# Moving one projection of an attention layer forward in a hand-ordered program, and two products of a hidden layer ahead of their two Relus

## The chip, the core and the metric

The kernel runs on one core of one Trainium2 chip. The metric is the device time of one execution in microseconds; lower is better. TensorE (PE in the profile) multiplies matrices into PSUM, VectorE (DVE) and ScalarE (ACT) read PSUM and work on SBUF, GpSimd (POOL) works on SBUF and issues some transfers, SyncE (SP) issues the other ones. Each engine runs its instructions in the order in which the program was written for it.

## What is computed

Eight sequences of 512 rows and 256 features go through two blocks. The first is a state-space layer: a projection to 512 channels, a short convolution, a recurrence over time with 16 states per channel, a gate and a projection back. The second is an attention layer of 16 heads whose values and outputs pass through 8 experts, of which the gates let 2 through, followed by a layer of 1024 hidden units (called the net below). In the reference, cut to what the change touches:

```python
q = _rope(einsum('bsd,hdp->bhsp', x, Wq))      # 16 heads of 64
k = _rope(einsum('bsd,hdp->bhsp', x, Wk))
v = einsum('bsd,bhse,hedp->bhsp', x, _gate(x, Wsel_v), Wv)
att = softmax(einsum('bhsp,bhtp->bhst', q, k) / sqrt(64))
o = einsum('bhst,bhtp->bhsp', att, v)
src2 = einsum('bhsp,bhse,hepd->bsd', o, _gate(x, Wsel_o), Wo)
...
src2 = relu(src @ W1 + b1) @ W2 + b2           # the net
```

`_rope` turns 32 of a head's 64 features by an angle that depends on the row: each feature is multiplied by a cosine, and a partner feature, multiplied by a sine, is added.

## The kernel before

**Work units.** Heads are taken in pairs, 8 pairs for each of the 8 sequences, 64 in all; pair 3.6 below is pair 6 of sequence 3. A pair consists of these parts, in the kernel's own numbering:

- the projection of q and k (`project`, L631): 8 matmul records on PE (L638). Then `turned` (L645) makes two products of its result on DVE, one with the sines (tile `sin`) and one with the cosines (tile `qk`), and `rotate` (L656) issues four transfers from POOL (L660) that add the rows of `sin` onto their partner rows of `qk`.
- v0 to v3 (`values`, L724): 8 matmul records each (L735). DVE multiplies the result by the gates into a tile `ve`, and POOL adds the eight experts up in three instructions (L750 to L752).
- s0 to s3 (`scores`, L667): 4 matmul records each (L676), which need the finished `qk`. DVE takes the row maximum (`low`), ACT the two exponentials (L691), DVE the reciprocal of the sum, ACT the scaling (L700).
- t0 to t3 (`turn_over`, L705): 8 transposes each (L711), copied out by ACT (L717).
- o (`attend`, L757): 16 matmul records (L764), which need all t and all v of the pair. ACT copies the result, and DVE multiplies it by the output gates in four steps (tile `og`, L785).
- a0 to a7 (`add_output`, L787): 4 matmul records each (L803), the output projection of the pair before. a0 and a1 need the first `og`, a2 and a3 the second, and so on.

**Order.** PE, DVE, ACT and POOL run exactly in the order in which the Python program emits their instructions. The attention parts are emitted in the list of `ahead` (L905); `following` in that list calls `follow` (L897), which emits the projection of q and k for the next pair. At the last pair of a sequence, `follow` first runs the planner until the next sequence is in `state` (L901): this is set (L599) when the last DVE instruction of `best(0)`, which makes the value gates `gv`, has been emitted.

After each part `order_of.run()` (class `_Order`) emits what has come due. Parts of the state-space layer, of the gates and of the net are generators that yield a waiting time; the planner counts PE time as the parts state it (`pe(3.42)`) and DVE time by the number of columns, and lets such a part go ahead while DVE is planned to be free at least 0.5 us before the next due step. ACT and POOL are not counted. The planner knows nothing of waits for buffers.

**Buffers.** All PE results except the output projection go into three PSUM buffers of `[128, 2, 512]` that are handed out in turn (`banks`, L274): a part may start to write when the reader of the third part before it is done. In SBUF there are two buffers in turn for each tag of the pool `work`. The four probability tiles `p` of a pair and `sin` share the tag "p"; the four `ve` tiles have the tag "ve". `qk` and `v` have one buffer.

**The net.** `feed_forward` (L812) takes the sequence before while the attention of the next one runs. Its hidden layer has 4 tiles of two products each per sequence (L853). Each product is followed by its Relu on ACT (L858), which writes half of tile `h`, and the part then yields 6.0. Two tiles are followed by the product with W2 (L868).

Of the kernel before, what the change touches and what calls it, by code (L numbers as in the profile page):

```python
# [25 lines left out]
F32 = mybir.dt.float32  # L26
# [5 lines left out]
P = 128  # L32
B, S, D = 8, 512, 256
# [6 lines left out]
NF = F // P  # L40
# [49 lines left out]
class _Order:  # L90
# [10 lines left out]
    def pe(self, us):  # L101
        self.now += us
        self.here = self.now
# [9 lines left out]
    def then(self, us, do):  # L113

        heapq.heappush(self.queue, (max(self.here, self.vec) + us, self.n, do))
        self.n += 1
# [84 lines left out]
def _layers(  # L201
# [4 lines left out]
    with ExitStack() as ctx:  # L206
# [6 lines left out]
        work = pool("work", 2)  # L213
# [60 lines left out]
        def banks(name):  # L274
            return psum.tile([P, 2, S], F32, tag="mm", name=name)

        def to_features(to, frm, name):

            ps = banks(f"ps_tr_{name}")
            for c in range(ND):  # L280
                for t in range(NT):
                    nc.tensor.transpose(ps[:, c, bass.ts(t, P)], frm[:, t, bass.ts(c, P)], ident)
            nc.scalar.copy(to, ps)
# [8 lines left out]
        pe, after, then = order_of.pe, order_of.after, order_of.then  # L292
# [324 lines left out]
        class Pair:  # L617
# [25 lines left out]
                after(0.05, lambda: self.turned(ps))  # L643

            def turned(self, ps):  # L645
                self.sin = work.tile([P, 2, S], F32, tag="p", name=f"sin_{self.id}")
                vector.tensor_tensor(
                    self.sin, ps, angle[:, 1].to_broadcast([P, 2, S]), ALU.mult
                )
                self.qk = one.tile([P, 2, S], F32, tag="qk", name=f"qk_{self.id}")  # L650
                vector.tensor_tensor(
                    self.qk, ps, angle[:, 0].to_broadcast([P, 2, S]), ALU.mult
                )
                then(0.0, self.rotate)
# [157 lines left out]
        def feed_forward(b, pa):  # L812

            xt, _ = state.pop(b)
            acc = big.tile([P, ND, S], F32, tag="big", name=f"acc_{b}")
            vector.tensor_tensor(acc, xt, pa, ALU.add)
            summed.add(b)
            yield 0.1
            while b + 1 < B and not (b + 1 in gated and (b + 2 == B or b + 2 in scanning)):
                yield 1.0  # L820
            ps = banks(f"ps_acc_{b}")
            ps = ps.rearrange("p a (t d) -> p (a t) d", d=D)
            for t in range(NT):
                for c in range(ND):
                    nc.tensor.transpose(ps[:, t, bass.ts(c, P)], acc[:, c, bass.ts(t, P)], ident)
            pe(1.05)
            y = big.tile([P, NT, D], F32, tag="big", name=f"y_{b}")
            nc.scalar.copy(y, ps)
            yield 1.2
            yield from norm(y, [y[:, t, :] for t in range(NT)])  # L830
            vector.tensor_tensor(y, y, g1, ALU.mult)
            yield 0.0
            vector.tensor_tensor(y, y, o1, ALU.add)
            yield 0.1
            yt = big.tile([P, ND, S], F32, tag="big", name=f"yt_{b}")
            to_features(yt, y, f"f_{b}")
            pe(1.05)
            yield 1.2
            b2 = half.tile([P, 1, D], F32, tag="half", name=f"b2_{b}")
            nc.sync.dma_start(out=b2[:, 0, :], in_=rows[:, 4 * D :].to_broadcast([P, D]))  # L840
            vector.tensor_tensor(y, y, b2.to_broadcast([P, NT, D]), ALU.add)

            for k in range(2):
                w = big.tile([P, ND, F // 2], F32, tag="big", name=f"w1_{b}_{k}")
                nc.sync.dma_start(out=w, in_=w1[:, :, k * F // 2 : (k + 1) * F // 2])
                hid = []
                for f in range(0, NF // 2, 2):
                    ps = banks(f"ps_f1_{b}_{k}_{f}")
                    h = big.tile([P, 2, S], F32, tag="big", name=f"hid_{b}_{k}_{f}")
                    for i in range(2):  # L850
                        at = k * NF // 2 + f + i
                        for c in range(ND):
                            nc.tensor.matmul(  # L853
                                ps[:, i, :], lhsT=w[:, c, bass.ts(f + i, P)], rhs=yt[:, c, :],
                                start=(c == 0), stop=(c == ND - 1),
                            )
                        pe(1.71)
                        nc.scalar.activation(  # L858
                            h[:, i, :], ps[:, i, :], AF.Relu, bias=b1_t[:, at : at + 1]
                        )  # L860
                    hid.append(h)
                    yield 6.0
                w = big.tile([P, NF // 2, D], F32, tag="big", name=f"w2_{b}_{k}")
                nc.sync.dma_start(out=w, in_=w2[:, k * NF // 2 : (k + 1) * NF // 2, :])
                ps = banks(f"ps_f2_{b}_{k}").rearrange("p a (t d) -> p (a t) d", d=D)
                for t in range(NT):
                    for f in range(NF // 2):
                        nc.tensor.matmul(  # L868
                            ps[:, t, :], lhsT=hid[f // 2][:, f % 2, bass.ts(t, P)], rhs=w[:, f, :],
                            start=(f == 0), stop=(f == NF // 2 - 1),  # L870
                        )
                    pe(1.71)
                    if t == 1:
                        yield 0.0
                yield 0.1
                vector.tensor_tensor(y, y, ps, ALU.add)
                yield 4.0
            z = big.tile([P, NT, D], F32, tag="big", name=f"z_{b}")
            x1 = big.tile([P, NT, D], F32, tag="big", name=f"x1_f_{b}")
            nc.sync.dma_start(out=x1, in_=x1_d[b])  # L880
            yield from norm(z, [y[:, t, :] for t in range(NT)])
            vector.tensor_tensor(z, z, g2, ALU.mult)
            yield 0.0
            vector.tensor_tensor(z, z, o2, ALU.add)
            yield 0.0
            yield from norm(z, [z[:, t, :] for t in range(NT)])
            vector.tensor_tensor(z, z, x1, ALU.add)
            nc.sync.dma_start(out=out[b].rearrange("(t p) d -> p t d", p=P), in_=z)
            finished.add(b)
# [15 lines left out]
        def ahead(n, following):  # L905


            for part in (
                "v0", "s0", 0, 1, "v1", "s1", 2, 3, "t0", "s2", "v2", "t1", "s3", 4, 5, "v3", "t2",
                following, 6, "t3", 7,  # L910
            ):
                if isinstance(part, int):
                    if last:
                        last.add_output(part)
                elif isinstance(part, str):
                    {"v": n.values, "s": n.scores, "t": n.turn_over}[part[0]](int(part[1]))
                else:
                    part()
                order_of.run()

        last = None
        with tc.manual_schedule(engines=MANUAL):
            first = front(0)
            order_of.start(first, 0, next(first))
            order_of.start(mamba(0), 0)
            first_constants()
            order_of.run(lambda: 0 in scanning)
            order_of.start(later_constants(), NET)
            order_of.run(lambda: 0 in state)
            pairs = {}  # L930
            follow(-1, H // 2 - 1)
            for b in range(B):
                for pair in range(H // 2):
                    now = pairs.pop((b, pair))
                    ahead(now, lambda: follow(b, pair))
                    if pair == 0 and b:
                        order_of.start(feed_forward(b - 1, sums[b - 1]), NET)
                    order_of.run(lambda: b in gated)
                    now.attend()
                    order_of.run()  # L940
                    last = now
            for k in range(E):
                last.add_output(k)
                order_of.run()
            order_of.start(feed_forward(B - 1, sums[B - 1]), NET)
            order_of.run(lambda: not (order_of.queue or order_of.rest))
# [83 lines left out]
```

## Time and profile before

| | us |
|---|---|
| runs shown: median (lowest to highest) | 3807.0 (3799.87 to 3809.49) |
| the profiled execution's own time | 3804.05 |
| its span, first to last instruction | 3802.3 |
| PE busy in the span | 3362.9 |
| DVE busy | 3049.0 |
| ACT busy | 1657.2 |
| POOL busy | 1656.8 |

The mean granted TensorE clock is 0.942 of full speed. A row of the groups names the line, the engine, the operation, what it writes and reads and how often it ran, then the busy time with the mean duration of one in ns, and then how long the engine had been idle just before these instructions and what ended that. In the view of waits a row is one kind of wait: who waited for whom, the sum, how often, and the longest. In a timeline, a row is a run of like instructions: start, length, engine, line, operation, and in brackets the idle time before it. All DVE instructions have the line of the helper that counts them (L160), so on DVE one goes by tile names.

The steps of an undisturbed pair, as the timeline shows them with PE at full clock: 3.4 us for a v part or the projection of q and k, 1.06 for an s part, 0.87 for a t part, 1.72 for an a part, 3.58 for o.

### The profile page before, as it was taken

The numbers are of one execution on the slowest core, as the hardware profiler recorded it, in microseconds if no ns is written. First come the engines' busy times: TensorE is split into PE (matmuls) and PEld (weight loads), VectorE is DVE, ScalarE is ACT, GpSimd is POOL, SyncE is SP. The second block draws the span as 40 slices with busy tenths as digits, with TensorE's granted clock in tenths as the row PEclk, the third lists the DMA queues.
The fourth block names the chain that finished last, engine by engine and source line by source line (L and its number), as shares of the span: only waits on it lengthen the run. The fifth ranks groups of instructions, "written<-read, shape, count | busy, mean of one in ns | idle before, by whom it ended". The sixth has DMA issues, their size and how long they took to land.

```text
span 3802.3 us, 33611 instructions
## 1 busy us (share of the span) xinstructions
PE 3362.9 (88%) x10464; PEld 1560.0 (41%) x10464; DVE 3049.0 (80%) x3218; ACT 1657.2 (44%) x2761; POOL 1656.8 (44%) x1601
## 2 busy tenths in 40 slices
PE   2039999399989999999999999999999999999996
PEld 0023444244444444444444444444444444444443
DVE  6976899799879888799878988799888989664432
ACT  4216654144544446444563446334463435332331
POOL 1323466255534545345443554445453557332220
PEclk6569999699999999999999999999999999999998
DMA  5934778368755867468674877557683777443431
GB/s 164 202 63 128 176 188 194 84 168 192 179 146 139 189 168 192 119 160 195 160 187 106 195 173 190 141 145 187 162 208 91 182 193 180 116 111 101 120 94 56
DMA packets 287760, 584.19 MB, mean 154 GB/s; under 512 B 37848, under 2 KB 125144, under 8 KB 287584
## 3 DMA queue, kind: packets, MB, share of 16 engines
q1 hardware_dynamic: 205664, 431.00, 38.3%
q0 software_dynamic: 81920, 151.04, 24.5%
q8 instruction: 85, 1.39, 0.1%
q14 instruction: 91, 0.75, 0.1%
HBM read 409.39 MB, written 21.51 MB: 113 GB/s over the span
## 4 chain that ended last, share of the span: by engine, by line
PE 57%; DVE 21%; DMA 7%; ACT 6%; issue 6%; POOL 3%; SPq 0%; DVEq 0%; POOLq 0%; ACTq 0%
PE ps_a L803 16%; PE ps_v L735 14%; DVE h L160 8%; PE ps_s L676 5%; PE ps_o L764 3%; PE ps_pt L711 3%; PE ps_f L853 3%; DMA xc<-h 3%; PE ps_qk L638 3%; PE ps_f L868 3%; DVE og L160 2%; DMA qk<-sin 2%; DVE ve L160 2%; PE ps_out L511 2%; DVE low L160 1%
## 5 line engine op out<-in xcount | busy, mean ns | idle before, releaser
L750 POOL TENSOR_TENSOR ve<-ve 128x512 f32<-128x512 f32 x256 | 420.2, 1641 | 1348.6 <-DVE ve L160 1248.0
L803 PE MATMUL ps_a<-og,wo 128*128 128x512 f32 x2048 | 978.5, 617 | 11.6 <-DVE og L160 11.2
L735 PE MATMUL ps_v<-wv,xt 128*128 128x512 f32 x2048 | 935.2, 599 | 3.8 <-ACT p L691 3.8
L160 DVE TENSOR_TENSOR_SCAN h<-da,h 128x1024 f32<-128x1024 f32 x256 | 609.7, 2382 | 87.1 <-ACT da L440 74.5
L691 ACT ACTIVATE p<-ps_s,low 128x512 f32<-128x512 f32 x512 | 347.3, 683 | 708.2 <-DVE low L160 707.7
L448 POOL DMA_DIRECT2D xc<-h x512 | 493.3, 1168 | 360.0 <-DMA xc<-h 145.6
L803 PEld LDWEIGHTS ps_a<-og,wo 128*128 128x128 f32 x2048 | 378.7, 195 | 547.4 <-issue 471.9
L735 PEld LDWEIGHTS ps_v<-wv,xt 128*128 128x128 f32 x2048 | 380.5, 191 | 517.0 <-issue 472.8
L700 ACT ACTIVATE p<-p,total 128x512 f32<-128x512 f32 x512 | 341.2, 714 | 190.5 <-DVE total L160 190.5
L160 DVE TENSOR_TENSOR og<-o,gb 128x1024 f32<-128x1024 f32 x256 | 311.6, 1238 | 118.2 <-ACT o L770 49.5
L160 DVE TENSOR_TENSOR ve<-ps_v,gv 128x1024 f32<-128x1024 f32 x256 | 311.4, 1216 | 117.4 <-PE ps_v L735 113.6
L717 ACT COPY pt<-ps_pt 128x1024 f32<-128x1024 f32 x256 | 256.7, 1003 | 334.8 <-PE ps_pt L711 334.1
L676 PE MATMUL ps_s<-qk 64*128 64x512 f32 x1024 | 328.8, 660 | 82.4 <-DMA qk<-sin 60.1
L440 ACT ACTIVATE da<-dt,decay 128x511 f32<-128x511 f32 x512 | 337.6, 713 | 140.9 <-DVE h L160 140.4
L160 DVE TENSOR_TENSOR h<-bt,dtx 128x1024 f32<-128x1024 f32 x256 | 345.1, 1348 | 17.6 <-DMA xc<-h 17.3
L160 DVE TENSOR_REDUCE low<-ps_s 128x2 f32<-128x1024 f32 x256 | 310.8, 1214 | 56.8 <-PE ps_s L676 55.9
L160 DVE TENSOR_TENSOR h<-h,ct 128x1024 f32<-128x1024 f32 x256 | 326.2, 1274 | 3.6
L751 POOL TENSOR_TENSOR ve<-ve 128x256 f32<-128x256 f32 x256 | 308.1, 1203 | 20.2
L660 POOL DMA_DIRECT2D qk<-sin x256 | 207.9, 1258 | 214.1 <-DVE qk L160 85.1
L711 PEld LDWEIGHTS ps_pt<-ident,p 128*128 128x128 f32 x2048 | 240.2, 142 | 133.9 <-issue 106.3
L711 PE MATMUL ps_pt<-ident,p 128*128 128x128 f32 x2048 | 267.5, 274 | 6.2 <-ACT pt L717 6.1
L511 PE MATMUL ps_out<-w_out,xc 128*128 128x256 f32 x256 | 66.5, 422 | 213.5 <-DVE xc L160 211.6
(114 smaller groups left out, 3271.9 us busy)
## 6 DMA issues: line engine op xcount, KB each, us to landing
xc<-h POOLq DMA_DIRECT2D x512, 256.0 KB, 5.7
gb<-go_d SPq DMA_DIRECT2D x512, 256.0 KB, 5.0
wv<-in_wv_dram SPq DMA_DIRECT2D x128, 512.0 KB, 4.6
wo<-in_wo_dram SPq DMA_DIRECT2D x512, 128.0 KB, 3.6
bt<-bc_d SPq DMA_DIRECT2D x64, 512.0 KB, 6.2
ct<-bc_d SPq DMA_DIRECT2D x64, 512.0 KB, 7.1
wqk<-wqk_d SPq DMA_DIRECT2D x64, 256.0 KB, 2.6
qk<-sin POOLq DMA_DIRECT2D x256, 64.0 KB, 4.4
```

The costliest lines, as they stand in the source:

```text
L160: return getattr(self.engine, name)(*args, **kw)
L440: nc.scalar.activation(das[k % 2][:, j, 1:S], dt[:, m, 1:S], AF.Exp, scale=decay[:, m, g + j : g + j + 1],)
L448: nc.gpsimd.dma_start(out=xc[:, k % NC, :], in_=h[:, j, :], accum_op=ALU.add)
L676: nc.tensor.matmul(ps[:, j, :], lhsT=self.qk[feats, 0, bass.ts(t, P)], rhs=self.qk[feats, 1, :], start=True, stop=True,)
L691: nc.scalar.activation(p[:, j, :], ps[:, j, :], AF.Exp, bias=low[:, j : j + 1], accum_out=total[:, j : j + 1],)
L700: nc.scalar.mul(p[:, j, :], p[:, j, :], total[:, j : j + 1])
L711: nc.tensor.transpose(pp[:, j, bass.ts(i, P)], self.p[t][:, j, bass.ts(i, P)], ident)
L717: nc.scalar.copy(self.pt[:, :, :, bass.ts(t, P)], pp.rearrange("p j (i q) -> p j i q", q=P))
L735: nc.tensor.matmul(ps[:, i, :], lhsT=self.xt[:, c, bass.ts(t + i, P)], rhs=self.wv[:, c, :], start=(c == 0), stop=(c == ND - 1),)
L750: nc.gpsimd.tensor_tensor(ve[:, :, 0:4], ve[:, :, 0:4], ve[:, :, 4:8], ALU.add)
L751: nc.gpsimd.tensor_tensor(ve[:, :, 0:2], ve[:, :, 0:2], ve[:, :, 2:4], ALU.add)
L803: nc.tensor.matmul(pa[:, c, :], lhsT=self.wo[:, i, bass.ts(c, P)], rhs=self.og[q][:, i, :], start=(self.pair == 0 and k == 0), stop=(self. ...
```

## The change

There are three edits. `sin` takes the tag "ve" in place of "p". In a tile of the net both products are emitted, 0.1 us of planner time passes, both Relus are emitted, and the part yields 4.0 in place of 6.0. In the list of parts the projection for the next pair (`following`) moves from behind t2 to right behind s3; a4 now stands between it and v3, and a5 between v3 and t2.

```diff
             def turned(self, ps):
-                self.sin = work.tile([P, 2, S], F32, tag="p", name=f"sin_{self.id}")
+                self.sin = work.tile([P, 2, S], F32, tag="ve", name=f"sin_{self.id}")
...
                     for i in range(2):
-                        at = k * NF // 2 + f + i
                         for c in range(ND):
                             nc.tensor.matmul(
                                 ps[:, i, :], lhsT=w[:, c, bass.ts(f + i, P)], rhs=yt[:, c, :],
                                 start=(c == 0), stop=(c == ND - 1),
                             )
-                        pe(1.71)
+                    pe(3.42)
+                    yield 0.1
+                    for i in range(2):
+                        at = k * NF // 2 + f + i
                         nc.scalar.activation(
                             h[:, i, :], ps[:, i, :], AF.Relu, bias=b1_t[:, at : at + 1]
                         )
                     hid.append(h)
-                    yield 6.0
+                    yield 4.0
...
             for part in (
-                "v0", "s0", 0, 1, "v1", "s1", 2, 3, "t0", "s2", "v2", "t1", "s3", 4, 5, "v3", "t2",
-                following, 6, "t3", 7,
+                "v0", "s0", 0, 1, "v1", "s1", 2, 3, "t0", "s2", "v2", "t1", "s3", following, 4,
+                "v3", 5, "t2", 6, "t3", 7,
             ):
```

The order of PE's parts from v2 of one pair to s0 of the next, before and after (qk is the projection):

```
before: v2 t1 s3 a4 a5 v3 t2 qk a6 t3 a7 o | v0 s0
after:  v2 t1 s3 qk a4 v3 a5 t2 a6 t3 a7 o | v0 s0
```

## The prediction

> **What bounds the kernel.** I read the page first, then PE's waits, then timelines of PE and DVE where the waits lie, then the granted clock there.
>
> ```profile
> span 3802.3 us, 33611 instructions
> PE 3362.9 (88%) x10464; PEld 1560.0 (41%) x10464; DVE 3049.0 (80%) x3218; ACT 1657.2 (44%) x2761; POOL 1656.8 (44%) x1601
> ```
>
> PE is the bound; it is idle for 439 us. Nearly half of that is one wait of 181 us at the start, which the change doesn't touch. Its waits, by cause:
>
> ```profile
> PE ps_out L511 <- DVE xc L160: 211.6, 5, 180.9
> PE ps_s L676 <- DMA qk<-sin: 60.1, 22, 22.1
> ...
> PE ps_f L853 <- ACT hid L858: 25.3, 32, 1.2
> ```
>
> The second row is s0 waiting for the turned q and k; 22.05 us of it is the very first pair (before any `ahead`), which leaves 38.0 in 21 waits. The third is the second product of a net tile waiting for the Relu of the first, 0.78 us, once for each of 32 tiles. A wait has a second price, the clock:
>
> ```profile
> 1473.90:1477.30 3.40, 3.40 (x5) 1.34 (x6) 3.00 (x5) 1.77 (x5) 2.57 (x4) 0.51 0.62 133
> 2009.90:2020.10 10.20, 8.65 (x10) 3.15 (x11) 8.98 (x12) 1.45 (x4) 5.14 (x4) 0.50 0.64 162
> 3573.00:3616.00 43.00, 43.00 (x138) 19.06 (x136) 17.33 (x18) 15.56 (x30) 12.92 (x16) 1.00 0.42 110
> ```
>
> The column before the DMA share is the granted clock. It is halved behind a q/k wait of 0.90 us at 1472.8 and for 10 us around one of 3.77 us at 2011.5; an unbroken stretch has 1.00. Half of PE's busy time in such a stretch is lost.
>
> Last, who is late where a sequence ends (4.0 begins at 2060.5), PE and then DVE:
>
> ```profile
> 2041.28 3.70 PE L803 MATMUL ps_a<-og,wo 128*128 128x512 f32 x8
> ...
> 2049.12 3.60 PE L638 MATMUL ps_qk<-xt,wqk 128*128 128x512 f32 x8
> ...
> 2068.42 1.19 PE L676 MATMUL ps_s<-qk 64*128 64x512 f32 x1 [4.18 <-DMA qk<-sin]
> ```
> ```profile
> 2057.89 0.69 DVE L160 TENSOR_TENSOR gv<-gv,hit 128x512 f32<-128x512 f32 x1
> 2058.50 3.38 DVE L160 RECIPROCAL s<-s 128x128 f32<-128x128 f32 x4
> 2061.80 1.16 DVE L160 TENSOR_TENSOR sin<-ps_qk,angle 128x1024 f32<-128x1024 f32 x1
> ...
> 2070.60 2.35 DVE L160 TENSOR_TENSOR og<-o,gb 128x1024 f32<-128x1024 f32 x2
> ```
>
> PE finished the projection at 2052.7, but the planner put all of `best(0)` ahead of `sin`, so DVE sets the pace here, not PE.
>
> **Relus.** No instruction is added. 32 stalls leave PE: −25.3. The chain of waits runs through these Relus (at 1707.86, for one), so the time is real. The buffer is now read until some 1.4 us after the second product (two Relus of 0.69) instead of 0.7; the third part behind it starts over 4 us later. The next tile comes 1.9 us of planner time sooner; its weights had not been waited for (0.3 us in all), and I cost this at nothing; uncovered it is that wait, once per load. If DVE paced these stretches, 10 of the 25 would be lost. I take **−25**.
>
> **q/k waits, ordinary pairs.** The projection comes 7.7 us of PE work earlier against s0 (1.72 + 3.43 + 1.72 + 0.87 for a4, v3, a5, t2). Every ordinary wait is shorter than that. Of the 38.0 us, 13.8 are at sequence starts (3.0 to 6.0) and 11.1 in three waits into pair 7 (2011.5, 2447.5, 2884.0), both below. The other 13.2 go, less 2.6 at four places where a0 then waits for the first `og`, which ended within 0.1 us of a0's start or within the wait: −10.6. Half-clock stretches behind them: four of 3.4 us busy and one of 6.2, half of 19.8: −9.9. Sum **−20.5**. The skill counts otherwise: "TensorE: Matmul & The Clock Gate", section "Why this matters for your kernels", lets PE idle up to about 3 us between bursts before the clock falls. By that rule none of these waits (at most 2.78 us) costs clock, and the sum is −10.6. The row with 0.51 behind 0.90 us speaks against it, so I keep −20.5.
>
> **The new bank wait.** Three PSUM buffers go round. The projection now takes the one v2 filled, with only t1 and s3 between (1.93 us from v2's end to s3's end), and waits until DVE has made `ve` of v2. Before, v3 took it, 5.6 us behind. Single instructions, pair by pair: `ve` of v2 ends 1.26 to 1.4 us after v2 in half the pairs, and later than s3's end in 11 of the 56 pairs that aren't a sixth pair; the excess sums to 7.8 us. All of PE queues behind it. With DVE 0.6 us later the sum is 17.9, with 1.2 us 42.9; below nothing it can't be, an added wait gives nothing. I take 7.8 as measured, and 3 for three half-clock stretches: **+11**. The other turns are covered: v3 takes t1's buffer (an ACT copy of 1.0 us, 6.2 us behind), t2 takes s3's (11 behind), t3 the projection's (two DVE products of 1.2, over 10 behind).
>
> **POOL.** The four transfers now stand ahead of v3's three adds; who waits for those is o. They take 3.2 us from first to last and start 0.56 after `qk`, so in a prompt pair they end 9.6 us after s3 (3.44 for the projection, 2.40 for DVE, 0.56, 3.2), and `ve` of v3 at 9.9 (3.44 + 1.72 + 3.43 + 1.26): no delay. A late pair loses up to 2.6. From v3's end to o there are now 6.9 us instead of 8.55; o reads the last v 2.3 us after its start. The adds end up to 11.4 us after v3 today; what exceeds 9.2 sums to 12.6, half of it in sixth pairs, and to 57.9 if each comes 2.6 later. I take half the first and a little for late pairs: **+8**. SP loads `wqk` one place earlier, ahead of a4's `wo`; its buffer has been free for a pair, and PE's wait for it is 0.0. `sin` in "ve" follows v1's adds, and v3's `ve` now follows v2's, which end at most 6.5 us after `ve` of v2 against over 9 to v3's. Next pair's v0 waits for transfers issued over 10 us before. Nothing; were POOL later still, DVE would wait in its place.
>
> **Pairs 6.** ACT holds DVE up behind the state-space projection (`h` waits 7.88 us for `da` at 1992). Today s0 waits 3.8 and runs at half clock; after it, the projection would wait 3.4 for v2's `ve` (1980.0 against 1976.6). From 1980.0: projection 3.4, a4 1.7, the state-space projection 7.0, v3 3.4, then a5, t2, a6, t3, a7 6.9 bring o to 2002.4; it waits about 2 for v3's `ve`, which stands behind the same `h`. Then o, v0 and s0 (8.3) put a0 at 2012.7, and some half clock at 2014, against 2015.4 today: −1 each, **−3** for 3.6, 4.6 and 5.6.
>
> **Sequence starts.** `follow` blocks the planner with 7.7 us less PE work emitted. From one `gv` to the next `follow` it emits the same PE parts and the same DVE work as before, so DVE's rest at `follow` stays: 4.5, 6.0 and three times 9.5 us (last `gv` minus start of the projection). The first `og` ends 13.2 us after that `gv`; now four more parts (7.9 in planner units) are between, 21.1. Rest plus 21.1 gives s3 to a0: 25.6, 27.1, 30.6. Today's are 25.6, 27.1 and 30.7 to 30.9. So **0** for 2.0 to 6.0, and 7.0 has no rest. At 1.0 DVE's `gv` (750.6) is fixed by the scans, and the parts that today run before the 51 us of stall run after it: 7.9, less 1.2 for v3's `ve` now behind, and a little clock: **+8**.
>
> **Sum.** −25 − 20.5 + 11 + 8 − 3 + 0 + 8 = −21.5 on the profiled execution's 3804.05 gives 3782.5; the median of the runs is 3 us higher, so 3785.5, forecast **3786**. A change under 0.3% (11 us) can't be told from none.
>
> **Rivals.**
> - *Blocked at each sequence start (slower).* If the rest at `follow` grows by the work no longer ahead of it, each of 2.0 to 6.0 pays 6.7 and some 3 of half clock: +49, so 3835. For it: a0 there starts within 0.5 us of the end of `og`, so DVE already decides. Against: the count above. It decides from 21.5/5 = 4.3 us per start on.
> - *Waits replaced.* POOL's transfers delay v3's adds in every second pair: +30 for +8, so 3807. For: nine sums of 10 us and more. Against: the prompt pair's order.
> - *All waits go.* No bank or POOL cost, and the waits into pair 7 vanish with their clock (11.1 + 12.3): −25 − 20.5 − 23.4 + 8 = −61, so 3746. Against: `ve` of v2 at 1980.0.
>
> **Chances.** Likeliest case 0.55 (own range 3768 to 3803; 0.43 of it faster, 0.11 same, 0.01 slower), blocked 0.20 (0.19 slower), replaced 0.13 (0.08 same, 0.04 slower), all go 0.12 (faster). Faster 0.56, same 0.20, slower 0.24. The range reaches to the centres of both outer cases, 3745 to 3835; half of each lies beyond.
>
> **What would show it.** Right: the row of `hid` gone from PE's waits, `qk<-sin` near 25 us, a new row ps_qk waiting for DVE `ve` of 10 to 20 us, fewer half-clock stretches between sequence starts. Wrong: ps_qk waits near 40; o waiting for POOL `v` over 20; s3 to a0 at 2.0 to 6.0 several us above today's; a net tile still with a gap.

## The result and the profile after

The changed kernel takes 3824.82 us (median of 4 runs, 3821.9 to 3828.83), the kernel before took 3803.98 beside it (4 runs, 3799.87 to 3809.49). The ratio is 1.0055 with the 95% interval [1.0041, 1.0068]: 21 us slower, where the forecast of 3786 us lies 18 us below before. The profiled execution of after has a span of 3824.7 us (before 3802.3), an own time of 3826.5 and a mean granted clock of 0.937 (0.942).

From the page of after, the span and the engines:

```profile
span 3824.7 us, 33541 instructions
PE 3344.8 (87%) x10464; PEld 1559.7 (41%) x10464; DVE 3065.8 (80%) x3218; ACT 1642.7 (43%) x2751; POOL 1682.4 (44%) x1601
```

PE's busy time is 18.1 us less for the same 10464 matmuls, but the span is 22.4 us more: PE stands still 40.5 us longer. PE's waits by cause, after:

```profile
PE ps_out L511 <- DVE xc L160: 218.5, 9, 181.9
PE ps_v L735 <- ACT p L691: 41.0, 8, 7.9
PE ps_o L764 <- POOL v L752: 34.9, 6, 13.3
...
PE ps_f L870 <- DMA w<-in_w_dram: 23.2, 10, 4.0
PE ps_s L676 <- DMA qk<-sin: 22.0, 1, 22.0
...
PE ps_go L608 <- DVE gt L160: 15.0, 8, 3.5
...
PE ps_f L852 <- DMA w<-in_w_dram: 9.9, 5, 2.4
...
PE ps_qk L638 <- DVE ve L160: 3.7, 9, 0.8
```

The row of `hid` is gone. `qk<-sin` has only the very first pair left. The bank wait of the projection (last row) is 3.7 us. All three are as wanted, or better. But other rows have grown. v waits for ACT's `p`, o for POOL's `v`, both products of the net for their weights (33.1 us where 0.3 had been), the transposes of L608 for `gt`, and o for ACT's `pt` (16.7 us where 3.6 had been; it is in the last line below).

The groups by line put the busy time and the wait of each kind of part side by side. Of after:

```profile
L735 PE MATMUL ps_v<-wv,xt 128*128 128x512 f32 x2048 | 954.9, 610 | 42.8 <-ACT p L691 41.0 <-ACT pt L717 1.6
L803 PE MATMUL ps_a<-og,wo 128*128 128x512 f32 x2048 | 954.7, 599 | 8.7 <-DVE og L160 8.2 <-DMA wo<-in_wo_dram 0.2
L676 PE MATMUL ps_s<-qk 64*128 64x512 f32 x1024 | 291.5, 643 | 27.1 <-DMA qk<-sin 22.0 <-ACT p L691 4.9 <-ACT sz L328 0.2
...
L764 PE MATMUL ps_o<-pt,v 128*64 128x512 f32 x1024 | 262.0, 638 | 51.7 <-POOL v L752 34.9 <-ACT pt L717 16.7
```

Of before:

```profile
L803 PE MATMUL ps_a<-og,wo 128*128 128x512 f32 x2048 | 978.5, 617 | 11.6 <-DVE og L160 11.2 <-DMA wo<-in_wo_dram 0.3
L735 PE MATMUL ps_v<-wv,xt 128*128 128x512 f32 x2048 | 935.2, 599 | 3.8 <-ACT p L691 3.8
L676 PE MATMUL ps_s<-qk 64*128 64x512 f32 x1024 | 328.8, 660 | 82.4 <-DMA qk<-sin 60.1 <-DVE top L160 13.2 <-ACT p L691 6.1
...
L764 PE MATMUL ps_o<-pt,v 128*64 128x512 f32 x1024 | 238.7, 602 | 4.1 <-ACT pt L717 3.6
```

Side by side:

| part | busy before, after | idle ahead of it before, after |
|---|---|---|
| s (L676) | 328.8, 291.5 | 82.4, 27.1 |
| a (L803) | 978.5, 954.7 | 11.6, 8.7 |
| v (L735) | 935.2, 954.9 | 3.8, 42.8 |
| o (L764) | 238.7, 262.0 | 4.1, 51.7 |

s and the a parts behind it lose 58 us of idle time and 61 us of busy time (the four records of an s0 that had waited took 3.91 us at 2068.4 in before, at a granted clock of 0.50, where 1.06 is usual). v and o pay 87 us of idle time and 43 of busy time. The waits have been moved to other parts, not removed.

The clock, in the columns of the prediction's windows:

```profile
1915.70:1919.10 3.40, 3.40 (x10) 0.96 (x8) 1.06 (x2) 0.00 (x0) 0.17 (x1) 0.50 1.05 231
1998.90:2005.20 6.30, 6.28 (x9) 2.66 (x10) 2.96 (x9) 4.77 (x9) 0.00 (x0) 0.56 0.30 86
2083.90:2088.60 4.70, 4.70 (x9) 1.76 (x8) 4.70 (x5) 1.81 (x3) 1.78 (x2) 0.74 0.77 199
```

The first is an o that had waited 2.46 us for ACT's `pt`, the second the v2 that had waited for `p`, the third the v0 behind the waits for POOL and for `gt`. Summed over the trace PE works 161.8 us where the granted clock is 0.5, 151.1 before: half clock has changed its place too, from s and a to v and o, and has not become less.

**Where the time goes.** From the first s0 of a sequence to the next, before and after:

| sequence | 0 | 1 | 2 | 3 | 4 | 5 | 6 | 7 to the end |
|---|---|---|---|---|---|---|---|---|
| before | 477.6 | 435.1 | 437.6 | 435.5 | 436.5 | 435.0 | 406.5 | 455.8 |
| after | 477.3 | 442.3 | 441.7 | 443.7 | 443.6 | 443.7 | 400.5 | 448.3 |

The loss is 35 us, in sequences 1 to 5; the last two gain 13.5. In the mean of sequences 2 to 5, PE's busy time falls from 419.2 to 418.0 us and its idle time rises from 17.0 to 25.2. Of the 25.2, v waits 7.9 for `p`, the net 6.5 for weights, o 4.3 for POOL and 2.5 for ACT's `pt`, and L608 1.8 for `gt`. The three largest, in the timelines.

*v for `p`.* PE, then DVE, after:

```profile
1978.12 6.31 PE L511 MATMUL ps_out<-w_out,xc 128*128 128x256 f32 x28 [1.26 <-DVE xc L160]
...
1989.92 1.13 PE L676 MATMUL ps_s<-qk 64*128 64x512 f32 x4
1998.92 6.42 PE L735 MATMUL ps_v<-wv,xt 128*128 128x512 f32 x8 [7.87 <-ACT p L691]
```
```profile
1980.31 1.22 DVE L160 TENSOR_TENSOR h<-bt,dtx 128x1024 f32<-128x1024 f32 x1
1989.19 2.29 DVE L160 TENSOR_TENSOR_SCAN h<-da,h 128x1024 f32<-128x1024 f32 x1 [7.66 <-ACT da L440]
...
1996.19 1.20 DVE L160 TENSOR_REDUCE low<-ps_s 128x2 f32<-128x1024 f32 x1
```

The state-space projection (L511) ends; ACT copies it (1984.47), scales `xc` (2.56 us) and only then makes `da`. DVE's scan waits 7.66 us for that, and the row maximum of s1, `low`, stands behind the scan. ACT's `p` needs `low`, and v2 needs the PSUM buffer that `p` reads: PE waits 7.87 us. The same block of DVE is in before (7.88 us at 1992). There L511 ran between a5 and v3 in sequences 3 to 5; in after it runs between v1 and s1, in all of sequences 1 to 5.

*o for POOL's `v`.* At the start of sequence 4, PE, POOL and DVE:

```profile
2070.38 2.79 PE L764 MATMUL ps_o<-pt,v 128*64 128x512 f32 x10
2077.48 3.67 PE L764 MATMUL ps_o<-pt,v 128*64 128x512 f32 x6 [4.32 <-POOL v L752]
2082.98 1.11 PE L608 MATMUL ps_go<-ident,gt 128*128 128x128 f32 x4 [1.82 <-DVE gt L160]
```
```profile
2070.65 3.19 POOL L660 DMA_DIRECT2D qk<-sin  x4 [12.90 <-PE ps_a L803]
2073.80 1.63 POOL L750 TENSOR_TENSOR ve<-ve 128x512 f32<-128x512 f32 x1
2075.51 1.05 POOL L751 TENSOR_TENSOR ve<-ve 128x256 f32<-128x256 f32 x1
2076.65 0.78 POOL L752 TENSOR_TENSOR v<-ve 128x128 f32<-128x128 f32 x1
```
```profile
2064.49 3.38 DVE L160 RECIPROCAL s<-s 128x128 f32<-128x128 f32 x4
2067.79 1.16 DVE L160 TENSOR_TENSOR sin<-ps_qk,angle 128x1024 f32<-128x1024 f32 x1
...
2072.50 1.22 DVE L160 TENSOR_TENSOR ve<-ps_v,gv 128x1024 f32<-128x1024 f32 x1
```

The four transfers stand ahead of v3's adds on POOL, but they are not what the adds wait for. They end at 2073.84, and the product `ve` that the adds read is done on DVE at 2073.72. So the transfers hold the adds up by some 0.1 us. DVE is late: PE has finished v3 at 2063.5, and its product stands behind the value gates, four reciprocals, `sin`, `qk` and four instructions of the output gates. At all six starts the adds begin within 0.15 us of the end of `ve`.

*Weights.* The net in sequence 4, PE, and SP at its second load of W2 (L866):

```profile
2201.69 3.60 PE L852 MATMUL ps_f<-yt,w 128*128 128x512 f32 x8
...
2209.70 3.70 PE L803 MATMUL ps_a<-og,wo 128*128 128x512 f32 x8
2217.36 7.93 PE L870 MATMUL ps_f<-w,hid 128*128 128x256 f32 x23 [3.96 <-DMA w<-in_w_dram]
```
```profile
2208.65 1.18 SPq L779 DMA_DIRECT2D gb<-go_d  x2
2209.88 0.59 SPq L866 DMA_DIRECT2D w<-in_w_dram  x1
```

The load is issued at 2209.88, behind loads of `gb`; PE is ready for it 3.5 us later and stands for 3.96. So this load took 7.5 us. (The profile has a landing for 10 of the 32 loads of the net's weights, with a median of 7.2 us; in before for 4, with a median of 4.8.) In before the same load was issued 14 us ahead of its product, SP and then PE:

```profile
2199.62 0.47 SPq L864 DMA_DIRECT2D w<-in_w_dram  x1
```
```profile
2213.58 7.07 PE L868 MATMUL ps_f<-w,hid 128*128 128x256 f32 x32
```

### The profile page after: what moved, and what is told of

The parts are those of the page before. It is cut to its first block, busy times and chain, and to the rows that moved or that the text cites. A ratio compares the mean times of both kernels' runs of the same rounds, so it can differ in the third digit from the quotient of the medians.

```text
span 3824.7 us, 33541 instructions
## 1 busy us (share of the span) xinstructions
PE 3344.8 (87%) x10464; PEld 1559.7 (41%) x10464; DVE 3065.8 (80%) x3218; ACT 1642.7 (43%) x2751; POOL 1682.4 (44%) x1601
## 4 chain that ended last, share of the span: by engine, by line
PE 56%; DVE 22%; DMA 8%; ACT 6%; issue 5%; POOL 3%; SPq 0%; DVEq 0%; POOLq 0%; ACTq 0%
PE ps_v L735 17%; PE ps_a L803 14%; DVE h L160 9%; PE ps_qk L638 5%; PE ps_s L676 4%; DMA xc<-h 3%; PE ps_pt L711 3%; PE ps_o L764 3%; PE ps_f L870 2%; DMA w<-in_w_dram 2%; PE ps_in L316 2%; DVE og L160 2%; DVE hit L160 2%; PE ps_out L511 1%; DVE ve L160 1%
## 5 line engine op out<-in xcount | busy, mean ns | idle before, releaser
L735 PE MATMUL ps_v<-wv,xt 128*128 128x512 f32 x2048 | 954.9, 610 | 42.8 <-ACT p L691 41.0
L803 PE MATMUL ps_a<-og,wo 128*128 128x512 f32 x2048 | 954.7, 599 | 8.7 <-DVE og L160 8.2
L750 POOL TENSOR_TENSOR ve<-ve 128x512 f32<-128x512 f32 x256 | 431.7, 1686 | 1156.1 <-DVE ve L160 1015.2
L448 POOL DMA_DIRECT2D xc<-h x512 | 467.5, 1072 | 468.7 <-DVE h L160 234.9
L160 DVE TENSOR_TENSOR_SCAN h<-da,h 128x1024 f32<-128x1024 f32 x256 | 599.1, 2340 | 74.0 <-ACT da L440 61.4
L735 PEld LDWEIGHTS ps_v<-wv,xt 128*128 128x128 f32 x2048 | 389.0, 195 | 570.0 <-issue 494.5
L803 PEld LDWEIGHTS ps_a<-og,wo 128*128 128x128 f32 x2048 | 368.3, 190 | 473.4 <-issue 423.5
L160 DVE TENSOR_TENSOR h<-bt,dtx 128x1024 f32<-128x1024 f32 x256 | 350.9, 1371 | 30.9 <-DMA xc<-h 30.9
L676 PE MATMUL ps_s<-qk 64*128 64x512 f32 x1024 | 291.5, 643 | 27.1 <-DMA qk<-sin 22.0
L764 PE MATMUL ps_o<-pt,v 128*64 128x512 f32 x1024 | 262.0, 638 | 51.7 <-POOL v L752 34.9
```

Of the source, the lines that this page charges most:

```text
L160: return getattr(self.engine, name)(*args, **kw)
L448: nc.gpsimd.dma_start(out=xc[:, k % NC, :], in_=h[:, j, :], accum_op=ALU.add)
L676: nc.tensor.matmul(ps[:, j, :], lhsT=self.qk[feats, 0, bass.ts(t, P)], rhs=self.qk[feats, 1, :], start=True, stop=True,)
L735: nc.tensor.matmul(ps[:, i, :], lhsT=self.xt[:, c, bass.ts(t + i, P)], rhs=self.wv[:, c, :], start=(c == 0), stop=(c == ND - 1),)
L750: nc.gpsimd.tensor_tensor(ve[:, :, 0:4], ve[:, :, 0:4], ve[:, :, 4:8], ALU.add)
L764: nc.tensor.matmul(po[j * HP : j * HP + HP, 0, :], lhsT=self.v[:, j, t, :], rhs=self.pt[:, j, t, :], start=(t == 0), stop=(t == NT - 1),)
```

## The experiments

Each kernel was timed beside the kernel before, whose median lay between 3803.98 and 3806.15. Ratios are to before, with 95% intervals.

### The parts by themselves

Three places were suspected: the sequence starts, where o waits for v3's adds (A1 in the expectations); the early next tile of the net, whose weights come late; and the part of PE's order behind which the state-space projection is emitted (P). First each edit was run alone.

net_only: the edit of the net. 

> Only the net's edit: both products, then both Relus, and a yield of 4.0 in place of 6.0; the projection and the sines stay as before. Theory A (the waits of each edit add up): the 25.3 us of waits for the first Relu go, but the tiles of W1 and W2 are asked for earlier than their buffers and loads allow, which in the changed kernel's profile cost PE 33 us; so +3 to +12 us, about 3812. Theory B (DVE's chain through the state-space layer sets the length of a sequence, PE's waits are only where it shows): within 6 us of before.

net_late: the same with a later next tile.

```diff
-                    yield 4.0
+                    yield 5.9
```


> The net's edit with a yield of 5.9 behind the Relus, so that the next tile comes at the planned time of before (0.1 + 5.9 = 6.0). Theory A: waits for W1 and W2 fall back to nearly nothing and the 25 us are gained, 15 to 25 us faster, about 3783. Theory B: within 6 us of before.

move_only: the new list of parts and the tag, the old net. 

> Only the projection's move, with the sines in the tag of the weighted values; the net as before. Theory A: the changed kernel's +21 us less the net's share, so +9 to +18 us, about 3818, with o waiting for POOL's v at sequence starts (some 4 us each) and a wait of some 8 us at pair 7. Theory B: all of the +21 us is here, 3822 to 3828, with 443 us from sequence to sequence.

tag_only: 

> Only the tag of the sines; order and net as before. Both theories: within 4 us of before, since neither buffer of either tag was waited for by PE beyond 0.5 us; a larger loss would mean that v0 of the next pair now waits for the transfers that read the sines.

both_late: the changed kernel with `yield 5.9`. 

> The changed kernel with one number altered: the net's part yields 5.9 behind the Relus in place of 4.0. Theory A (the edits' costs add up: the Relu pairing gives 24 us as measured alone, the early W1 and W2 loads take them back, the move costs 11): 3815 - 24 = 3791 +- 6, and PE's waits for W1 and W2 under 5 us in place of 33. Theory B (DVE's chain sets the length of a sequence once the projection is moved): still above 3808, with 440 us or more from sequence to sequence.

| kernel | us | ratio |
|---|---|---|
| net_only | 3803.66 | 0.9995 [0.9987, 1.0002] |
| net_late | 3780.32 | 0.9921 [0.9902, 0.994] |
| move_only | 3815.21 | 1.0025 [1.0017, 1.0032] |
| tag_only | 3804.39 | 0.9999 [0.9991, 1.0008] |
| both_late | 3791.73 | 0.9966 [0.9952, 0.9979] |

Pairing the Relus is worth 24 us (net_late to before) and 23.5 on top of the move (both_late to move_only). The shorter yield takes that back: 23 us alone (net_only to net_late), 33 with the move (after to both_late). The move by itself costs 10.6 us, the tag nothing. So the 21 us of the whole are −24 for the Relus, +23 for the 4.0, +11 for the move, and another +11 that only shows when the 4.0 and the move meet.

In net_only PE's waits show one row that neither before nor net_late has:

```profile
PE ps_f L870 <- DMA w<-in_w_dram: 22.1, 5, 5.5
```

22.1 us of waits for W2, against 23 us of time between net_only and net_late, in which the state-space projection stands behind the same parts. (o's waits for `pt` are longer too, 16.7 us against 3.6, but they stay, at 18.1, in net_early_w2 below, which is fast.) Between after and both_late the waits for weights are 33.1 and 2.7 us, the times 33 apart.

### The load of W2

How long before its product is the load of W2 issued? From the trace, for the second W2 product in sequences 3 to 6: the start of the product minus the start of its load on SP, less PE's wait.

| kernel | PE ready behind the issue by | PE then waits |
|---|---|---|
| before | 13.9 to 14.4 | 0 |
| net_late | 8.5 | 0 |
| net_only | 2.8 | 4.2 to 5.5 |
| after | 3.5 to 4.9 | 2.0 to 4.0 |

The program emits the load right ahead of the product. It is early only by as much as SP runs ahead of PE, and on SP it stands behind other loads. net_early_w2 keeps the 4.0 and asks for W2 ahead of the second tile; after_early_w2 does that in the changed kernel.

```diff
                 for f in range(0, NF // 2, 2):
+                    if f:
+                        w_2 = big.tile([P, NF // 2, D], F32, tag="big", name=f"w2_{b}_{k}")
+                        nc.sync.dma_start(out=w_2, in_=w2[:, k * NF // 2 : (k + 1) * NF // 2, :])
...
-                w = big.tile([P, NF // 2, D], F32, tag="big", name=f"w2_{b}_{k}")
-                nc.sync.dma_start(out=w, in_=w2[:, k * NF // 2 : (k + 1) * NF // 2, :])
+                w = w_2
```

> Only the net's edit with its 4.0, but the tile of W2 is asked for and loaded before the second hidden tile in place of behind it. If the loads of W2 are what 4.0 costs (PE waits 22 us for them there, and the gain of 24 us is missing): those waits under 5 us and 12 to 25 us faster than before, about 3785. If 4.0 costs something else (the place where the net's parts land): still within 6 us of 3804.

> The changed kernel with W2 asked for before the second hidden tile. If the loads alone are the difference of 33 us to the same kernel with 5.9: 3792 to 3805, with the weights' waits under 12 us (W1's stay). If they only account for what they account for in the net's edit alone: 3800 to 3812. If the landing places decide: within 8 us of 3825.

net_early_w2 took 3770.22 us, 0.9911 [0.989, 0.9932]: 33 less than net_only. after_early_w2 took 3804.45, 0.9997 [0.9985, 1.0009]: 20 less than after, and no slower than before. PE is now ready 15 to 17 us behind the issue, and no W2 product waits in either. So asking earlier gives back 20 of the 33 us that the 4.0 costs beside the move; the other 13 are not accounted for. The waits for W1 stay at 9.9 us (2.7 in both_late), and the state-space projection stands at another place than in both_late, which is taken up below. With the load of W2 cured the changed kernel is still 34 us behind net_early_w2: that is the move.

### The move, by places

move_not_last moves the projection at pairs 0 to 6 only, move_last_only at pair 7 only (both with the old net, as has the next one).

```diff
+            tail = (
+                following, 4, "v3", 5, "t2", 6, "t3", 7
+            ) if n.pair < H // 2 - 1 else (
+                4, 5, "v3", "t2", following, 6, "t3", 7
+            )
...
```


> The move (and the sines' tag) for pairs 0 to 6 of a sequence only; at pair 7, where the projection belongs to the next sequence and has to wait for its gates to be emitted, it stays behind t2. Net as before. Theory A1 (the move's cost lies at the sequence starts: o waiting for POOL's v, then PE waiting for gt): 8 to 20 us faster than the whole move, 3795 to 3807, and o's waits for POOL's v under 5 us. Theory A2 (the cost is spread over the ordinary pairs): within 5 us of the whole move's 3815 or above it.

> The opposite: the move at pair 7 only, elsewhere the old order. Theory A1: slower than before by 8 to 20 us, 3813 to 3825, with the waits of o for POOL's v (some 13 us at 1.0 and 3 to 4 each after it) and for gt. Theory A2: within 4 us of before. My forecast's own term (8 us at 1.0 and nothing at the later starts) gives 3812.

move_behind_v3 puts it behind v3, so that POOL's adds come first.

```diff
-                "v0", "s0", 0, 1, "v1", "s1", 2, 3, "t0", "s2", "v2", "t1", "s3", 4, 5, "v3", "t2",
-                following, 6, "t3", 7,
+                "v0", "s0", 0, 1, "v1", "s1", 2, 3, "t0", "s2", "v2", "t1", "s3", 4, "v3", following,
+                5, "t2", 6, "t3", 7,
```


> The projection between v3 and a5 for all pairs (order: s3, a4, v3, projection, a5, t2, a6, t3, a7, o), so that v3's product on DVE and its adds on POOL stand ahead of the sines and of the four transfers. Net as before. If v's lateness at o behind DVE's rest and POOL's transfers is the cost: o's wait for POOL's v under 5 us in all and 5 to 15 us faster than the whole move, near 3803. If the cost is that less PE work stands ahead of the blocked step: within 5 us of the whole move's 3815.

after_v3_first is the changed kernel with that order at pair 7 alone. 

> The changed kernel, but at pair 7 alone the projection stands behind v3 (s3, a4, v3, projection, a5, t2, ...), so that DVE and POOL have v3's product and adds in front of the gates' rest, the sines and the four transfers. If o's wait for POOL's v at the sequence starts (4.3 us, then 1.8 for gt, at half clock: some 8 us in five sequences) is time on the path: 15 to 40 us faster than the changed kernel, 3785 to 3810. If it is only where DVE's lateness shows: within 8 us of 3825, with the wait back at s0 or a0.

| kernel | us | ratio |
|---|---|---|
| move_not_last | 3839.33 | 1.0088 [1.0073, 1.0102] |
| move_last_only | 3801.88 | 0.9992 [0.9983, 1.0001] |
| move_behind_v3 | 3803.87 | 1.0003 [0.9992, 1.0013] |
| after_v3_first | 3832.39 | 1.0073 [1.006, 1.0087] |

The move at the sequence ends alone costs nothing, and the move everywhere else costs more (35 us) than the whole (10.6). So, with the old net, the loss doesn't come from the starts. after_v3_first says the same of the changed kernel: PE's wait for POOL's `v` is gone, and the kernel is no faster (8 us slower by the medians; the intervals overlap). What stands in its place, in PE's waits:

```profile
PE ps_v L735 <- ACT p L691: 41.1, 8, 7.9
PE ps_a L803 <- DVE og L160: 36.2, 18, 5.3
PE ps_o L764 <- ACT pt L717: 32.9, 12, 5.6
PE ps_f L870 <- DMA w<-in_w_dram: 28.4, 11, 4.5
```

In after the second and third of these are 8.2 and 16.7. So A1, the loss at the starts, falls, although PE's stretch there does get longer (see "Sequence starts" below). move_behind_v3 is as fast as before: put behind v3 in every pair, with the old net, the projection costs nothing. That is what its expectation had for v3's lateness as the cause (near 3803). But waits of 35.2 us for `qk`, 41.2 for `og` and 14.7 for W1 stand in this kernel, and the state-space projection changes its place too, so it doesn't show which of these decides.

### The block of DVE behind the state-space projection

Behind which part the state-space projection is emitted differs from kernel to kernel. In sequences 3 to 5, with PE's idle time and half of its time at half clock, in the 51 us from 6 us ahead of it:

| kernel | the projection stands between | idle + half clock, us |
|---|---|---|
| before | a5 and v3 | 8.3, 8.7, 7.1 |
| net_late | a5 and v3 | 7.1, 7.9, 8.2 |
| move_only | a1 and v1 | 5.9, 9.2, 5.9 |
| move_not_last | v1 and s1 | 16.1, 15.4, 13.0 |
| after | v1 and s1 | 11.9, 12.2, 12.2 |
| late_fix | v3 and t2 | 4.4, 2.0, 3.7 |

The two kernels with the place between v1 and s1 are the slowest of the six. By the same measure, after_early_w2 (between v1 and s1) loses 16 us more than both_late (between a1 and v1) over sequences 1 to 5. That could be the 13 us left open above; no run tests it. The scan that waits some 7.7 us for `da` can be put off, so that other DVE work goes ahead of it:

```diff
-                yield 0.0
+                yield 5.0 if b and k == 0 else 0.0
```

This was added to four other kernels and to the changed one: before_fix to before, not_last_fix to move_not_last, late_fix to net_late, both_late_fix to both_late, after_fix to after.

> The kernel before with the same 5.0. Theory P: its projection lands between a5 and v3, where the block costs less (3.8 us of wait at s0 and half clock behind it, three times): 5 to 20 us faster, 3785 to 3800. Theory S: within 5 us of before.

> The kernel with the move at pairs 0 to 6 only (3839) with the same 5.0. It too has the projection between v1 and s1 with four waits of 7.87 us. Theory P: 20 to 45 us faster, 3795 to 3820. Theory S: within 8 us of 3839.

> The net's edit with 5.9 (3780 alone) and the same 5.0, without the move: a candidate that beats both kernels. Theory P: 5 to 20 us faster than 3780. Theory S: within 5 us of 3780.

> The changed kernel with the net's 5.9 and the 5.0 before the first scan. If the net's price is independent of the rest (24 us in both pairs of kernels so far): 3821 - 24 = 3797 +- 8. If the 5.0 had already removed it (the weights' waits are gone from that kernel's profile): within 8 us of 3821.

> The changed kernel plus one number: in the recurrence of sequence b the first scan is emitted 5.0 us of planner time after its two decays (0.0 before), so that DVE isn't planned into the stretch in which ACT still copies the previous state-space projection and scales xc (DVE's first scan waits 7.7 us for da there, in every kernel so far). Theory P (what the move really changes is the place among PE's parts where the state-space projection lands; in the changed kernel it lands between v1 and s1, and the blocked DVE then holds s1's and s2's rows, so that PE waits 7.87 us for p at v2 in five sequences): those five waits go, 20 to 45 us faster than the changed kernel's 3825. Theory S (spread: the q/k waits only come back elsewhere, wherever the projection lands): within 8 us of 3825.

| kernel | us | ratio to before | less than without it | DVE's waits for `da`, without and with it |
|---|---|---|---|---|
| before_fix | 3774.62 | 0.9923 [0.991, 0.9936] | 31 | 74.5, 37.3 |
| not_last_fix | 3795.8 | 0.9974 [0.9964, 0.9984] | 44 | 62.3, 26.2 |
| late_fix | 3754.79 | 0.9868 [0.9854, 0.9883] | 26 | 66.5, 36.0 |
| both_late_fix | 3781.79 | 0.9939 [0.9927, 0.9952] | 10 | 55.5, 53.1 |
| after_fix | 3821.57 | 1.0043 [1.0028, 1.0057] | 3 | 61.4, 28.9 |

The last column (us) shows that in both_late_fix the edit did not do what it was for: the scan still waits some 8 us for `da` in each of sequences 1 to 5. Of the four kernels that lose the block, wholly or in all sequences but one, three gain 26 to 44 us, and the changed one gains nothing clear. The edit also moves the state-space projection (to between v3 and t2 in most sequences of before_fix and late_fix, to between a3 and t0 in after_fix and both_late_fix), so the block and the place are not told apart. In after_fix too the wait for `p` is gone; PE's waits:

```profile
PE ps_out L511 <- DVE xc L160: 236.8, 9, 182.0
PE ps_o L764 <- POOL v L752: 41.8, 6, 13.3
PE ps_a L803 <- DVE og L160: 37.0, 16, 5.1
...
PE ps_o L764 <- ACT pt L717: 21.8, 7, 3.7
```

40 us of waits for `p` have left; `og` has gained 29, `ps_out` 18, POOL 7, `pt` 5. There is no wait for weights left in this kernel either, and yet it is 40 us behind both_late_fix, from which only the 4.0 parts it. What the 4.0 costs there is neither a wait for W2 nor the place, which is the same in both in sequences 1 to 5, and stays open.

Two more kernels. after_out_later holds the state-space projection back:

```diff
+            if b:
+                yield 7.0
```


> The changed kernel with 7.0 us of planner time more before the state-space layer's out projection from the second sequence on, which should put it between s2 and v2 in place of v1 and s1, where two sequences of another kernel lost 0.8 us around it against 9 here. Theory P (the landing place decides): the 7.87 us waits at v2 go, and 10 to 40 us faster than 3825 although the chain to the gates is 7 us longer. Theory S: not faster than 3820.

It took 3858.55, 1.0134 [1.0116, 1.0152]: 34 us more than after, though the waits of 7.87 us are gone. The edit missed the place that it was for. In sequences 2 to 5 the state-space projection fell behind s3, half of it ahead of the projection of q and k and half behind, and the scan's wait for `da` grew to 11.5 or 12.2 us, from 7.66 in after. Only in sequence 1 did it stand between s2 and v2, and there the scan waited 10.0. So this run says little on that place. all_cures has 5.9, 5.0 and v3 first at pair 7. 

> The changed kernel with the net's 5.9, the 5.0 before the first scan, and the projection behind v3 at pair 7. If the three prices found (weights, blocked scan, v3 behind the transfers at the sequence starts) explain why the move loses, this reaches the same two cures without the move (3755) within 12 us. If the move itself is a loss beyond them: above 3775.

 It took 3796.77, 0.9977 [0.9967, 0.9987], 15 more than both_late_fix. So P, too, holds only in part: taking that block away pays 26 to 44 us in three kernels, and the block alone doesn't explain the changed kernel.

late_fix, the net's edit with 5.9 and the put-off scan, and without the move, is the fastest kernel here: 50 us below before and 70 below after.

## Why the prediction was wrong

**The step that failed** is in "Relus": "The next tile comes 1.9 us of planner time sooner; its weights had not been waited for (0.3 us in all), and I cost this at nothing; uncovered it is that wait, once per load". The 0.3 us said that the loads came in time; it did not say by how much. The trace of before had the answer, the 14 us between the issue of the second load of W2 and its product, and the prediction didn't read it. Pairing the products alone shortens it to 8.5 (net_late), the 4.0 to 2.8 (net_only), under the 7.0 to 8.3 that the load then took. Price: 23 us alone, where asking earlier for W2 took all of it away again, and 33 with the move, where it took 20 away. What the text named as the price if uncovered, the wait for a load, is what the rows show (22.1 us in 5 waits for W2, 33.1 in 15 for W1 and W2). A second step failed at the sequence starts, below.

**Relus, the gain.** Right: −25 was predicted, −24 and −23.5 were measured where the 4.0 is left out, and the row of `hid` is gone.

**q/k waits.** The waits went, all 38.1 us of them (the sum counted 10.6), and s and a took 61 us less busy time (9.9 counted, as half clock). The mechanism was right and its size too small; but it is not a gain of time, since the wait came back at v and o with its half clock. The sign of fewer half-clock stretches did not come (161.8 us of PE's work at 0.5, before 151.1).

**Bank wait.** Predicted +11, measured 3.7 us. One premise was wrong: t3 ran at 2067.69 while DVE read the projection's bank until 2070.0, so the buffers are not taken strictly in turn, as the text had it. How much of the difference this makes is not shown.

**POOL.** Predicted +8, bound 57.9; the waits of o for POOL's `v` are 34.9 us, 13.3 of which at the first start take the place of 13.2 of s0. The other 21.6 are 4.3 at each of five starts: the sign "over 20" for wrong is met. But the mechanism of this term, the transfers ahead of the adds, costs some 0.1 us at these starts; the wait is that of v3's product on DVE. Curing it gave nothing back (after_v3_first).

**Pairs 6.** Predicted −3. The projection of the state-space layer was taken to stay behind a4; it came between v1 and s1. By the table of places that is 36.3 us for the three sequences where before had 24.1: +12 where −3 was predicted.

**Sequence starts.** 0 was predicted for 2.0 to 6.0. From s3 to a0, between which the same attention parts run before and after, PE took 36.3, 34.9, 35.0, 35.1 and 35.2 us; before it was 25.7, 27.1, 31.0, 30.9 and 30.8. That is 31 us more, and the sign "several us above today's" is met. The count of DVE's rest at `follow` held at three starts: it is 9.9 us at each (before 4.5, 6.0 and three times 9.5), so it grew by 5.4 and 3.9 at two. What the count left out is that v3's product stands behind the gates at these starts too, where o waits 4.32 us for it and L608 1.8 more for `gt`; it had taken 1.2 for this, at 1.0 alone. What the 31 us are worth is another matter. after_v3_first brings the five stretches to 28.9 us each, 32 less than in after, and the five stretches between the starts become 32 longer.

The rival of *blocked starts* needed 6.7 us more of rest at each. In move_last_only the same five stretches take 16 us more than in before and the kernel is no slower, so it isn't by itself what made the kernel slower. *Waits replaced* came nearer: waits were replaced, but by others than v3's adds behind the transfers. At 1.0 the predicted +8 did not come: sequence 0 is as long as before.

**The sum of the move.** −20.5 + 11 + 8 − 3 + 8 is +3.5; move_only measured +10.6, and the move costs 11 us with the old net or with 5.9, 21 with 4.0, 27 with 5.9 and the put-off scan, and 34 with 4.0 and W2 early. Of after_early_w2 the groups show where it is paid:

```profile
L735 PE MATMUL ps_v<-wv,xt 128*128 128x512 f32 x2048 | 956.9, 611 | 53.7 <-ACT p L691 39.5 <-DVE y L160 12.4 <-ACT pt L717 1.6
...
L764 PE MATMUL ps_o<-pt,v 128*64 128x512 f32 x1024 | 259.1, 629 | 50.1 <-POOL v L752 34.9 <-ACT pt L717 15.1
```

Against net_early_w2, which has all but the move, v waits 47 us more and o 32, s 51 less. Taking any one of these waits away (after_fix, after_v3_first, after_out_later) let others grow. One reading, argued and not shown, is that DVE sets the pace. In all these kernels it works 380 to 385 us per sequence (mean of sequences 2 to 5); the rest is its own standing behind heads of line (an instruction that waits and holds up all behind it) such as the scan that waits for `da`; and where the parts of PE stand only decides which of PE's instructions meets that. A sequence takes 436.2 us before and 443.2 after. Of these 7 us, 3 are more work of DVE in as many instructions, and 4 more standing. Why the moved order brings them is not settled.

## What to carry to other kernels

A wait of 0 says that a transfer is in time, not by how much: before bringing its consumer forward, read the time from its issue to its use, and compare it with its landing. Where several engines wait for each other in order, a wait removed from one engine is time gained only if the others were not about to be late in the same stretch; follow each removed wait to the next one before counting it. Run the parts of an edit by themselves: here one edit was worth 24 us, and the 4.0 and the move took 45 back.

## What the runs showed of the hardware

Half clock followed a wait of only 2.46 us ahead of 1915.0 in after: the granted clock was 0.50 from 1915.7 to 1919.1. Yet it did not follow a wait of 3.40 us ahead of 3105.0 in the same trace:

```profile
3105.00:3108.40 3.40, 3.40 (x16) 3.01 (x17) 3.37 (x4) 1.81 (x5) 3.32 (x4) 1.00 1.07 302
```

So the length of one wait didn't decide it here. At half clock an s part took 3.91 us, where 1.06 is usual. A load of the same 512 KB landed in 4.8 us (median of 4, before) and in 7.2 (median of 10, after). And executions of one and the same kernel scatter: net_only's lie between 3796 and 3814 us (the profiled one at 3811.86), and net_late's profiled one, 3764.32, lies 16 us below its median. So a difference between two single traces says little where the medians of the runs don't agree with it.
